# Filler and step banks counted apart, attention loads a tile ahead, C rows of 384 columns, the first step prepared first

## The chip, the cores and the metric

One core of a Trainium2 chip runs the whole program in one launch. The metric is the device time of one execution in microseconds (us). Engines are called as in the profile: PE (TensorE, matmuls), PEld (its weight loads), DVE (VectorE), ACT (ScalarE), POOL (GpSimd), SP (SyncE, which issues nearly all DMAs here). Everything below is of one core.

## The reference

The input x is 4 images of 512 channels by 64x64 positions. Two layers are added to it in turn.

```python
# layer 0: x = x + conv_ref(gn(x)); per position a layer norm over 512 channels, four chunks of 128 channels,
# each through a "mamba" (state 16, inner width 256, conv of 4 taps), a layer norm, a 512x512 projection
xz = in_proj(x);  xi, z = split(xz)
xc = silu(conv4(xi) + conv_b)
dt, Bs, Cs = split(xc @ x_proj_w.T);  dt = softplus(dt @ dt_proj_w.T + dt_proj_b)
h = exp(dt * A) * h + (dt * x) * B        # a scan over 4096 positions, for 256 channels x 16 states
y = sum_over_states(h * C)
y = (y + xc * D) * silu(z);  out = y @ out_proj_w.T
# layer 1: x = x + attn(gn(x)): linear attention with relu, 8 heads of 64
q, k, v = gn(x) @ w_qkv.T + b_qkv;  q, k = relu(q), relu(k)
kq = sum_over_positions(k^T q)  per head;   out = (v kq / kq.sum) @ w_out.T + b_out
```

gn is a group norm over a whole image. So the attention of an image can begin only when layer 0 has finished that whole image, and its second half only when kq has been summed over all positions.

## The kernel before

**Steps and slots.** Positions go in tiles of 512. A step is one chunk of 128 channels of one tile: 4 images x 8 tiles x 4 chunks = 128 steps (`steps`, `n`). A step has 16 slots (`SLOTS`, `s`); `slot` runs two scans (L596), and the next DVE product with the C row (`product`, L619, columns 0 to 383; the last 128 columns are multiplied by POOL, L607, with rows that come by DMA). For the scans ACT makes exp(dt A) in PSUM (`decay`, L570) and POOL makes dt x B (`drive`, L578). `c_row` spreads a row of C over the partitions by a bf16 matmul into a PSUM bank of its own (`ps_c`, 1 buffer), once every two slots, right behind the product that used the row before. `fold_states` sums the states by matmul into `y`.

**Around a slot.** The loop over steps is recorded in a fixed order (`manual_schedule`), engine by engine. Behind each slot, `after()` records the work of the next steps at set slots: `front` (the conv `pc`, two pieces each, and `pz`, of step n+2), `silu`, `mix` and `last_mix` (the piecewise `mixers`: `pd`, its copy to `dt` and `parts`, and two rounds of `minus` matmul and copy that split `parts` into bf16 pieces), `time_banks` (`pt`), `time_steps` (softplus, between two loads of ACT's table), `spread`, `gate`, `out_proj` (`po`), `with_skip`.

**Fillers.** What is not bound to a slot stands in four queues of generators and gets at most one piece per slot each: `ahead` (norm of the next tile), `late` (the layer norm and projection `pp` of the tile just done, `leave`), `rest` (attention), `light` (statistics of the next image). A generator yields "wait" when it can't go on: `room()` waits for a PSUM bank, `until()` for a piece that was recorded `later(2, ...)`, two slots on, `load()` for one of three x tiles (`TILES`), `pause(2)` for two slots. `credit` limits the matmuls per slot. Four PSUM banks (`ps_w`, `work_bank`, `free`, `held`) serve steps and fillers alike.

```python
limit[0] = 2 if s in (SLOTS - 1, 0, 5, 6) else BANKS - 1     # BANKS = 4; compared with held[0], all banks in use
```

**Attention of one image** (`attention`, in queue `rest`): pass a, over 8 tiles of 4 sub-tiles: load the tile (`xa`), pause, group norm on ACT, and for each sub-tile q and k (`pq`, a bias matmul and 4 f32 matmuls each), relu on ACT, and the sums k^T q (`pk`, 8 matmuls of 64x64, which read both relus), added to `kq` on DVE. Then a middle part (`pm2`, `pm3`, `pob`) folds kq and the weights into one 512x512 matrix. Pass b, over 8 tiles: load (`xb`), four outputs of 4 matmuls (`pr`), ACT adds the offset, SP stores.

**Before and behind the loop.** Before the loop, steps 0 and 1 are prepared (`step_inputs`, `silu`, `mixers`), then step 0's rows are spread and the first drives and decays are made. Behind the loop, the queues `late` and `rest` are simply emptied: `while late or rest: one(late) or one(rest)`; there a scheduler, and not the recorded order, places the instructions, `now[0]` is None, and nothing waits for a slot.

Of the kernel before, what the change touches and what calls it, by code (L numbers as in the profile page):

```python
# [24 lines left out]
def kernel(  # L25
# [49 lines left out]
    BANKS = 4  # L75
# [3 lines left out]
    def work_bank(name):  # L79
        held[0] += 1  # L80
        return ps_w.tile([P, T], F32, tag="w", name=name)
# [25 lines left out]
    def room():  # L107

        while now[0] is not None and held[0] >= limit[0]:
            yield "wait"  # L110

    limit, norming = [BANKS], []
# [11 lines left out]
    def load(src, name):  # L124

        while now[0] is not None and held_x[0] >= TILES:
            yield "wait"
        held_x[0] += 1
        xt = wk.tile([P, NC, T], F32, tag="x", name=name, bufs=TILES)
        nc.sync.dma_start(xt, src)  # L130
        return xt

# [193 lines left out]
    def layer_norm(v, name, gained):  # L326


        def means(parts, what, when):
            yield from room()  # L330
            sums = work_bank(f"{what}_sums_{name}")
            for c in range(NC):
                mm(
                    sums[c * LANE : (c + 1) * LANE, :], ones, parts[c],
                    start=True, stop=True, abreast=NC,
                )
            got = wk.tile([P, T], F32, tag="sq", name=f"{what}_got_{name}", bufs=4)

            def take():
                nc.scalar.copy(got, sums)  # L340
                free()

            copied = later(2, take)
            yield
            yield from until(copied)
            yield when
            yield from room()
            bank = work_bank(f"{what}_{name}")
            mm(bank, mean.to_broadcast([P, P]), got, start=True, stop=True)
            return bank  # L350

        while norming:
            yield "wait"
        norming.append(name)
        mu = yield from means([v[:, c, :] for c in range(NC)], "mu", "one ahead")
        yield "wide"
        nc.vector.tensor_tensor(v, v, bc(mu, NC), ALU.subtract)
        free()
        yield "free"
        sqs = []  # L360
        for c in range(NC):
            sqs.append(wk.tile([P, T], F32, tag="sq", name=f"sq_{name}_{c}", bufs=4))
            nc.scalar.activation(sqs[c], v[:, c, :], AF.Square)
            if c == 1:
                yield "free"
        var = yield from means(sqs, "var", "two ahead")
        rs = wk.tile([P, T], F32, tag="sq", name=f"rs_{name}", bufs=4)

        def root():
            nc.scalar.activation(rs, var, AF.Ln, bias=eps)  # L370
            nc.scalar.activation(var, rs, AF.Exp, scale=-0.5)

        rooted = later(2, root)
        yield
        yield from until(rooted)
        yield "wide"
        nc.vector.tensor_tensor(v, v, bc(var, NC), ALU.mult)  # L377
        free()
        norming.clear()
        yield  # L380
        if gained:
            for c in range(NC):
                nc.scalar.activation(
                    v[:, c, :], v[:, c, :], AF.Identity,
                    bias=b_sb[:, c : c + 1], scale=g_sb[:, c : c + 1],
                )
                if c % 2:
                    yield "free"
# [45 lines left out]
    def inputs(f, xn, c, nm):  # L434
# [11 lines left out]
        def take(e):  # L446
            nc.scalar.activation(xz[:, 0, e, :], pc[e], AF.Identity, bias=cb[:, e : e + 1])
            free()

        for e in range(NH):  # L450
            pc[e] = work_bank(f"pc_{nm}_{e}")
            taps(e, range(NTAP // 2))
            yield
            taps(e, range(NTAP // 2, NTAP))
            later(2, lambda e=e: take(e))
            yield
        for e in range(NH):
            pz = work_bank(f"pz_{nm}_{e}")
# [5 lines left out]
            def take_z(e=e, pz=pz):  # L464
                nc.scalar.copy(xz[:, 1, e, :], pz)  # L465
                free()

            later(2, take_z)

    def time_banks(f, nm):  # L470

        f["pt"] = [work_bank(f"pt_{nm}_{e}") for e in range(NH)]
# [4 lines left out]
    def time_steps(f, nm):  # L477
# [4 lines left out]
        free(NH)  # L482
# [18 lines left out]
    def mixers(f, nm):  # L501
# [3 lines left out]
        pd = work_bank(f"pd_{nm}")  # L505
# [12 lines left out]
        parts = f["parts"] = wk.tile([P, T], BF16, tag="parts", name=f"parts_{nm}", bufs=2)  # L518
        nc.scalar.copy(parts, pd)
        for i in (2, 3):  # L520
            yield
            mm(pd, minus, parts, start=False, stop=True, skip_group_check=True)
            yield
            nc.scalar.copy(parts[i * LANE :, :], pd[i * LANE :, :])  # L524
        free()
# [33 lines left out]
    def c_row(g):  # L559
        n, e, q, _ = place(g)  # L560
        got = ps_c.tile([P, T], F32, tag="c", name=f"c_all_{g}")
# [52 lines left out]
    def product(g, last):  # L614
# [4 lines left out]
        nc.vector.tensor_tensor(own, own, bc(c_all[g // JJ][:, :CUT], 2), ALU.mult)  # L619
# [27 lines left out]
    def out_proj(f, nm):  # L647
        f["po"] = work_bank(f"po_{nm}")
# [3 lines left out]
    def with_skip(f, xn, c):  # L652
        v = xn[:, c, NTAP - 1 : NTAP - 1 + T]
        nc.vector.scalar_tensor_tensor(v, v, sk, f["po"], ALU.mult, ALU.add)
        free()
# [13 lines left out]
    def attention(b, x1s, norm):  # L669
# [4 lines left out]
        qk = both[:, 1:3, :].rearrange("p j c -> p (j c)")  # L674

        def relu(j, pq):
            nc.scalar.activation(qk[:, j * C : (j + 1) * C], pq, AF.Relu)  # L677
            free()
# [8 lines left out]
        for t in range(NT):  # L687
            gn = yield from load(x1s[t], f"xa_{b}_{t}")
            yield
            yield from pause(2)  # L690
            yield "free"
            yield from group_norm(gn, gn, norm)
            for u in range(SUB):
                nm = f"{b}_{t}_{u}"
                ready = []
                for j in range(2):
                    yield from room()
                    pq = work_bank(f"pq_{nm}_{j}")
                    mm(
                        pq, sel[:, 0, 0:1].to_broadcast([P, P]), bqk[:, j * C : (j + 1) * C],  # L700
                        start=True, stop=False,
                    )
                    for c in range(NC):
                        mm(
                            pq, gn[:, c, u * P : (u + 1) * P], w_qk[:, c, j * C : (j + 1) * C],
                            start=False, stop=(c == NC - 1),
                        )
                        if c == 1:
                            yield "more"
                    ready.append(later(2, lambda j=j, pq=pq: relu(j, pq)))  # L710
                    yield
                yield from until(*ready)
                yield from room()

                pk = work_bank(f"pk_{nm}")[:, 0 : C // 2].rearrange("p (c d) -> p c d", c=NC)
                for p in range(NC):
                    for i in range(P // HEAD):
                        r = slice(p * P + i * HEAD, p * P + (i + 1) * HEAD)
                        mm(
                            pk[i * HEAD : (i + 1) * HEAD, p, :], qk[:, r], qk[:, C:][:, r],  # L720
                            start=(p == 0), stop=(p == NC - 1), skip_group_check=True,
                        )
                if u == SUB - 1:
                    later(1, free_x)
                added = later(2, lambda pk=pk, first=(t + u == 0): add(pk, first))
                yield
# [54 lines left out]
        yield from until(*taken)  # L781
        ob = small.tile([P, NC], F32, tag="ob", name=f"ob_{b}")
# [33 lines left out]
        for t in range(NT):  # L816
            x1 = yield from load(x1s[t], f"xb_{b}_{t}")
            yield
            yield from pause(2)
            for o in range(NC):  # L820
                yield from room()
                pp = work_bank(f"pr_{b}_{t}_{o}")
                for m in range(NC):
# [4 lines left out]
                    if m == 1:  # L828
                        yield "more"
                if o == NC - 1:  # L830
                    later(1, free_x)
                later(2, lambda t=t, o=o, pp=pp: store(t, o, pp))
# [32 lines left out]
    def leave(b, t):  # L865
# [8 lines left out]
        if t == NT - 1:  # L874
            yield
            norms[b, 1] = stats_end(stats1[b], f"b{b}")
            add_to(rest, attention(b, x1s[b], norms[b, 1]))
            yield
# [30 lines left out]
    for n in range(2):  # L909
        run(step_inputs(n))  # L910
        silu(n)
    run(mixers(fs[0], names[0]))
    time_banks(fs[0], names[0])
# [4 lines left out]
    run(mixers(fs[1], names[1]))  # L918
    nc.scalar.preload_act_table_set("natural_log_exp_and_others")
    for g in range(0, 3 * JJ, JJ):  # L920
        b_row(g)
    c_tail(0)
    c_row(0)
    for g in range(2):
        drive(g)
    for k in range(LEAD):
        decay(k)

    with tc.manual_schedule():
        credit, mix, held[0], held_x[0] = 0.0, iter(()), 0, 0  # L930
        for n, (b, t, c) in enumerate(steps):
# [10 lines left out]
            for s in range(SLOTS):  # L942
                def after():
# [10 lines left out]
                    if s < 3:  # L954
# [11 lines left out]
                    if s in (2, 4, 5, 6, 7):  # L966
# [10 lines left out]
                    if s == 5 and before is not None:  # L977
                        pb_, pt_, pc_ = steps[n - 1]
                        with_skip(before, xn[pb_, pt_], pc_)
                        if pc_ == NC - 1:  # L980
                            add_to(late, leave(pb_, pt_))
# [3 lines left out]
                    if s >= 13:  # L985
# [7 lines left out]
                    limit[0] = 2 if s in (SLOTS - 1, 0, 5, 6) else BANKS - 1  # L993
# [76 lines left out]
```

## Time and profile before

| | us |
|---|---|
| three runs | 8470.25, 8464.2, 8470.84; median 8470.25 |
| the profiled execution, its own time | 8479.35 |
| its span, first to last instruction | 8477.6 |
| busy: DVE / POOL / PE / ACT | 7348.7 / 6860.0 / 6672.1 / 5274.0 |
| first scan starts / last scan starts | 120.38 / 7840.67 |

The profile gives the shares of busy time in 40 slices of 212 us. The loop with its scans fills slices 1 to 37; the last slices hold attention alone. A line of the timeline or of the chain of waits begins with the start in us from the first instruction and the duration. Of the groups, a line gives the busy time, the mean duration of one in ns and the idle time of the engine before them, with what ended most of it. One f32 matmul of the source (128x512) stands in the trace as two matmul rows.

### The profile page before, as it was taken

How to read it: one execution, taken by the hardware profiler on the slowest of the kernel's cores; microseconds unless marked ns; L12 is line 12 of the kernel's file. 1: busy time of each engine (PE TensorE's matmuls, PEld its weight loads, DVE VectorE, ACT ScalarE, POOL GpSimd, SP SyncE). 2: the span in 40 equal slices, each digit the busy share in tenths (PEclk: the TensorE clock that was granted, in tenths of full speed). 3: DMA queues.
4: the chain of work that ended last, by engine and by line, in shares of the span. 5: the costliest groups of instructions: out<-in, count | busy, mean ns of one | idle time of the engine just before them, and what ended most of it. 6: DMA issues, size and time to landing. Idle time of an engine off the chain costs nothing. (4 is left out here: it accounts for less than half of the span.)

```text
span 8477.6 us, 86763 instructions
## 1 busy us (share of the span) xinstructions
PE 6672.1 (79%) x22169; PEld 2222.3 (26%) x22240; DVE 7348.7 (87%) x7097; ACT 5274.0 (62%) x7584; POOL 6860.0 (81%) x4565
## 2 busy tenths in 40 slices
PE   5677677777788888888888778888788888787999
PEld 1112121111222222222222222222222222222444
DVE  5999999999999999999999999999989999999000
ACT  4666666666666666666666766666666666665221
POOL 4999998999888888888888888888888898888000
PEclk8777787777888888888889998898888898888999
DMA  5666666566666665567666666566666666665202
GB/s 156 160 152 155 152 155 151 144 149 147 157 163 159 148 162 144 146 156 184 174 169 159 161 154 149 148 153 153 162 167 173 143 159 149 153 149 142 104 30 85
DMA packets 829304, 1266.14 MB, mean 149 GB/s; under 512 B 183920, under 2 KB 317568, under 8 KB 816512
## 3 DMA queue, kind: packets, MB, share of 16 engines
q1 hardware_dynamic: 821632, 1255.87, 59.3%
q10 hardware_dynamic: 7168, 4.71, 0.2%
q8 instruction: 174, 2.85, 0.2%
q14 instruction: 330, 2.70, 0.1%
HBM read 1053.28 MB, written 206.57 MB: 149 GB/s over the span
## 5 line engine op out<-in xcount | busy, mean ns | idle before, releaser
L578 POOL TENSOR_TENSOR bx<-d_all,b_all 128x1024 f32<-128x1024 f32 x2048 | 4795.8, 2360 | 113.6 <-DVE h L596 97.4
L596 DVE TENSOR_TENSOR_SCAN h<-dA,st,bx 128x512 f32<-128x512 f32 x3584 | 4457.2, 1274 | 273.5 <-ACT dA L570 199.7
L570 ACT ACTIVATE dA<-d_all,a_t 128x512 f32<-128x512 f32 x4096 | 2800.5, 689 | 2384.2 <-DVE h L596 2371.6
L619 DVE TENSOR_TENSOR h<-h,c_all 128x768 f32<-128x768 f32 x2048 | 1915.7, 935 | 73.2 <-PE c_all L120 63.8
L120 PE MATMUL c_all<-parts,sel 128*128 128x512 bf16 x1024 | 458.8, 448 | 1252.6 <-DVE h L619 1250.5
L120 PE MATMUL y<-h,fold 128*32 128x512 f32 x8192 | 1378.0, 752 | 62.0 <-POOL h L607 60.7
L607 POOL TENSOR_TENSOR h<-h,c_sb 128x512 f32<-128x512 f32 x1024 | 1298.1, 1268 | 116.1 <-DMA c_sb<-c_rows 29.0
L120 PE MATMUL pc<-xn,w_cv 128*128 128x512 f32 x2048 | 1051.6, 645 | 21.4 <-ACT parts L524 13.8
L120 PE MATMUL pq<-w_qk,xa 128*128 128x512 f32 x2048 | 980.5, 608 | 8.7 <-issue 6.6
L606 POOL COPY st<-h 128x4 f32<-128x4 f32 x1024 | 192.4, 188 | 638.1 <-DVE h L596 589.5
L596 DVE TENSOR_TENSOR_SCAN h<-dA,bx 128x512 f32<-128x512 f32 x512 | 605.3, 1211 | 92.1 <-POOL bx L578 48.0
L120 PEld LDWEIGHTS <-sel 128*128 128x128 bf16 x1280 | 126.2, 99 | 2125.8 <-DVE h L619 1944.6
L120 PEld LDWEIGHTS pc<-xn,w_cv 128*128 128x128 f32 x2048 | 396.2, 206 | 742.8 <-issue 650.0
L120 PEld LDWEIGHTS pq<-w_qk,xa 128*128 128x128 f32 x2048 | 397.8, 196 | 483.1 <-issue 471.0
L120 PE MATMUL pp<-xn,w_pr 128*128 128x512 f32 x1024 | 516.5, 633 | 7.5 <-DVE xn L377 3.8
L120 PE MATMUL pr<-xb,m 128*128 128x512 f32 x1024 | 495.5, 629 | 13.8 <-ACT xz L465 7.1
L120 PE MATMUL y<-xz,dg 128*128 128x512 f32 x512 | 391.2, 858 | 0.0
L120 PEld LDWEIGHTS y<-h,fold 128*32 128x32 f32 x8192 | 175.8, 118 | 686.7 <-issue 400.1
L643 POOL TENSOR_TENSOR xz<-xz 128x512 f32<-128x512 f32 x256 | 325.0, 1270 | 1.8 <-ACT xz L640 1.8
L487 POOL TENSOR_TENSOR dt<-dt,xz 128x1024 f32<-128x1024 f32 x128 | 302.5, 2363 | 24.4 <-ACT dt L479 24.4
L677 ACT ACTIVATE kq<-pq 128x512 f32<-128x512 f32 x256 | 150.2, 587 | 247.0 <-PE pq L120 246.5
L120 PE MATMUL pd<-parts,minus 128*128 128x512 bf16 x256 | 121.0, 473 | 230.3 <-ACT parts L524 147.7
(151 smaller groups left out, 6159.4 us busy)
## 6 DMA issues: line engine op xcount, KB each, us to landing
d_all<-d_rows SPq DMA_DIRECT2D x2048, 256.0 KB, 6.6
b_all<-b_rows SPq DMA_DIRECT2D x4096, 64.0 KB, 2.2
d_rows<-dt SPq DMA_DIRECT2D x256, 512.0 KB, 3.4
c_sb<-c_rows SPq DMA_DIRECT2D x4096, 16.0 KB, 1.8
xs<-in_x_dram SPq DMA_DIRECT2D x32, 1024.0 KB, 7.7
xn<-in_x_dram SPq DMA_DIRECT2D x32, 1024.0 KB, 6.0
xr<-in_x_dram SPq DMA_DIRECT2D x32, 1024.0 KB, 6.9
x<-xr SPq DMA_DIRECT2D x32, 1024.0 KB, 4.2
```

The costliest lines, as they stand in the source:

```text
L120: nc.tensor.matmul(out_, lhsT, rhs, **how)
L487: nc.gpsimd.tensor_tensor(f["both"][:, 1], f["both"][:, 0], f["xz"][:, 0], ALU.mult)
L570: nc.scalar.activation(dAs[k], fs[n]["d_all", e][:, 0, j, :], AF.Exp, scale=a_t[:, e, j, q : q + 1])
L578: nc.gpsimd.tensor_tensor(bxs[g], fs[n]["d_all", e][:, 1, jj * 2 : jj * 2 + 2, :], bc(b_all[g // JJ], 2), ALU.mult)
L596: nc.vector.tensor_tensor_scan(h[:, j, :], dAs.pop(2 * g + i), bxs[g][:, i, :], 0.0 if t == 0 else st[:, c, e, q, j : j + 1], ALU.mult, AL ...
L606: nc.gpsimd.tensor_copy(st[:, c, e, q, :], h[:, :, T - 1])
L607: nc.gpsimd.tensor_tensor(h[:, :, CUT:], h[:, :, CUT:], bc(c_sb.pop(g // JJ), NJ), ALU.mult)
L619: nc.vector.tensor_tensor(own, own, bc(c_all[g // JJ][:, :CUT], 2), ALU.mult)
L643: nc.gpsimd.tensor_tensor(f["xz"][:, 1, e, :], f["xz"][:, 1, e, :], f["xz"][:, 0, e, :], ALU.mult)
L677: nc.scalar.activation(qk[:, j * C : (j + 1) * C], pq, AF.Relu)
```

## The change

The diff, cut to what is spoken of. The step's own banks are no longer counted; fillers count theirs, against a new limit. In attention the x tiles are fetched by the piece before they are needed, and the sums of a sub-tile are recorded behind the next sub-tile's q (three relu buffers instead of two). The statistics of an image are ended inside `attention`, behind the first fetch. The C row, `parts` and their matmuls have 384 columns. `with_skip` is recorded before the conv piece of its slot, `pz` is cut in two pieces (slots 7 and 8), and `mix` starts one slot earlier. Before the loop, step 0 goes the whole way before step 1 is begun.

```diff
-    BANKS = 4
-    def work_bank(name):
-        held[0] += 1
+    def work_bank(name, behind=1):
+        held[0] += behind
...
+    def no_tile():
+        return now[0] is not None and held_x[0] >= TILES
+
+    def load_now(src, name):
         held_x[0] += 1
         xt = wk.tile([P, NC, T], F32, tag="x", name=name, bufs=TILES)
         nc.sync.dma_start(xt, src)
         return xt
...
-            pc[e] = work_bank(f"pc_{nm}_{e}")
+            pc[e] = work_bank(f"pc_{nm}_{e}", 0)
...
+            later(2, lambda e=e, pz=pz: nc.scalar.copy(xz[:, 1, e, :], pz))
+            yield
...
-        parts = f["parts"] = wk.tile([P, T], BF16, tag="parts", name=f"parts_{nm}", bufs=2)
-        nc.scalar.copy(parts, pd)
+        parts = f["parts"] = wk.tile([P, CUT], BF16, tag="parts", name=f"parts_{nm}", bufs=2)
+        nc.scalar.copy(parts, pd[:, :CUT])
...
-        got = ps_c.tile([P, T], F32, tag="c", name=f"c_all_{g}")
+        got = ps_c.tile([P, CUT], F32, tag="c", name=f"c_all_{g}")
...
+        def fetch(t, why):
+            if t < NT and t not in tiles and not no_tile():
+                x1 = load_now(x1s[t], f"x{why}_{b}_{t}")
+                tiles[t] = x1, pause(2)
+
+        def fetched(t, why):
+            fetch(t, why)
+            while t not in tiles:
+                yield "wait"
+                fetch(t, why)
+            x1, landing = tiles.pop(t)
+            yield from landing
+            return x1
...
-        for t in range(NT):
-            gn = yield from load(x1s[t], f"xa_{b}_{t}")
-            yield
-            yield from pause(2)
...
-                yield from until(*ready)
-                yield from room()
...
+        fetch(0, "a")
+        yield
+        norm = stats_end(stats, f"b{b}")
+        yield
+        for v in range(NT * SUB):
+            t, u = divmod(v, SUB)
...
+                qk[i] = both[:, 1 + i % 3, :]
+                ready[i] = later(2, lambda i=i, pq=pq: relu(i, pq))
+                if u:
+                    fetch(t + 1, "a")
...
+                if v and j == 0:
+                    yield from sums(v - 1)
                     yield
...
+        fetch(0, "b")
...
-            x1 = yield from load(x1s[t], f"xb_{b}_{t}")
-            yield
-            yield from pause(2)
+            x1 = yield from fetched(t, "b")
...
+                fetch(t + 1, "b")
...
-    for n in range(2):
-        run(step_inputs(n))
-        silu(n)
+    run(step_inputs(0))
+    silu(0)
     run(mixers(fs[0], names[0]))
+    b_row(0)
+    c_tail(0)
...
     for g in range(2):
         drive(g)
+    run(step_inputs(1))
+    silu(1)
+    run(mixers(fs[1], names[1]))
...
-                    if s < 3:
+                    if s < 2:
                         next(last_mix, None)
...
-                    if s in (2, 4, 5, 6, 7):
+                    if s in (2, 4, 5, 6, 7, 8):
                         next(front, None)
...
-                    if s >= 13:
+                    if s >= 12:
                         next(mix, None)
...
-                    limit[0] = 2 if s in (SLOTS - 1, 0, 5, 6) else BANKS - 1
+                    limit[0] = 3 if 9 <= s < 13 else 2
```

## The prediction, made before the changed kernel had run

> **What bounds the kernel now.** I read first the busy shares over the 40 slices, to see which engine sets the pace where:
>
> ```profile
> PE   5677677777788888888888778888788888787999
> DVE  5999999999999999999999999999989999999000
> ```
>
> For 37 slices DVE is at nine tenths and sets the pace; then it is at nothing, and PE at nine tenths is alone. So there are two kernels to price: a loop of 2048 slots bound by DVE, where matmuls cost only what they delay, and a stretch behind it bound by PE. The chain of waits that ended last shows what stands in that stretch:
>
> ```profile
> 7899.11 2.31 issue
> 7901.42 19.10 PE pm L120 x40
> 7920.52 11.08 PE pob L120 x64
> 7931.59 112.56 PE pr L120 x256
> 8044.17 5.65 DMA xa<-x
> 8049.85 2.22 ACT xa L315 x3
> ```
>
> An image has one middle part and 256 rows of `pr`, and here they come twice: before 8044 they are those of image 2, whose attention was not done when the loop ended; image 3 begins only at 8049.85. Third, the windows by image (columns: window, its length, then busy us and count of PE, PEld, DVE, ACT, POOL, granted clock, DMA share, GB/s):
>
> ```profile
> 120.00:2002.00 1882.00, 1326.91 (x4030) 365.35 (x4030) 1799.61 (x1696) 1232.30 (x1748) 1710.81 (x1136) 0.78 0.63 152
> 2002.00:3949.00 1947.00, 1567.98 (x5373) 519.58 (x5391) 1837.61 (x1766) 1300.83 (x1874) 1715.20 (x1140) 0.86 0.63 156
> 3949.00:5901.00 1952.00, 1573.31 (x5394) 520.16 (x5410) 1833.98 (x1759) 1308.00 (x1887) 1715.92 (x1141) 0.88 0.64 159
> 5901.00:7844.00 1943.00, 1564.41 (x5348) 521.47 (x5371) 1804.82 (x1713) 1278.06 (x1844) 1708.24 (x1135) 0.88 0.63 155
> ```
>
> DVE is idle for window less busy: 82, 109, 118 and 138 us. Image 0 has no attention beside it; the three others have one each, and pay 27, 36 and 56 us of idle DVE for it. Last, whom DVE waits for in these three images (us in total, times, longest):
>
> ```profile
> DVE h L596 <- ACT dA L570: 181.2, 103, 4.9
> DVE h L619 <- PE c_all L120: 63.8, 58, 4.3
> DVE h L596 <- POOL h L607: 27.6, 25, 1.8
> ```
>
> ACT's exp that comes late is the first, the C row that stands behind other matmuls the second.
>
> **Part 1, image 2's attention leaves the end.** I counted in the order of the two built programs' PE instructions, by C rows (1024, one for two slots). Before, pass a of images 0, 1 and 2 begins at C rows 284, 565 and 853; each takes some 280 rows for the 256 that an image has, so it falls behind, and at row 1024 the last sums, the middle part and all of pass b of image 2 are left. After, they run over rows 282 to 466, 538 to 722 and 794 to 976: 184 rows each, ending 48 rows early. So the removed waits (two slots for the relus of each sub-tile, load and pause for each tile, room that step banks took away) are real, and the left-over goes. Image 3's start is then set by its own group norm:
>
> ```profile
> 7888.61 0.16 DVE L309 TENSOR_TENSOR off_b<-ngm_b,gr_b 128x4 f32<-128x4 f32 x1 [1.12 <-POOL gr_b L305]
> ```
>
> It is ready at 7888.77, and ACT starts its first tile at 8049.82: with the load of tile 0 issued before the statistics, these 161 us go. The cover is the loop; its price is part 4.
>
> **Part 2, sums behind the next q, at the end.** In pass a of image 3 each sub-tile takes 8.83 us (two are 17.67 in the chain), and holds one stall:
>
> ```profile
> 8096.78 0.69 PE L120 MATMUL pk<-kq 128*64 128x64 f32 x16 [0.74 <-ACT kq L677]
> ```
>
> `pk` waits 0.74 us for the relu of its k. Behind the next q, some 4 us later, that relu (0.60 us) is done. 31 of 32 sub-tiles have a next q: 31 x 0.74 = 23 us, all on the path, since PE alone is busy there. ACT has 51 us of work in these 274 us and can't become the bound; the middle part and pass b (112.8 us of `pr` without a gap) stay.
>
> **Part 3, step 0 first.** Step 1's matmuls and copies stood before step 0's `dt` copy; silu of step 0 ends at 89.47 and that copy starts at 96.68. So step 0's rows go out some 5 us earlier. But ACT now does step 1's copies and silu before the first exps, which came at 114.12: by my count from the durations there they come at about 115.5, and the first scan at about 116.5 instead of 120.38. I take 4 us off; ends are 8 off (drive alone decides) and 2 on.
>
> **Part 4, the loop.** (a) PE gets 172 units more (a unit is one f32 128x512 matmul of the source): 1315 instead of 1143 of attention, and it gets them denser: some 51 units per step over some 70 steps, where before 46 were spread over 92; then 26 steps have none. Busiest before were steps of 53 units:
>
> ```profile
> 5042.00:5105.00 63.00, 54.69 (x177) 18.53 (x176) 60.25 (x60) 40.43 (x57) 53.36 (x35) 0.86 0.60 144
> ```
>
> There PE is busy 54.7 of 63 us, 1.03 us a unit, and DVE idles 2.8 us: no more than the 2.6 us of a step without attention (82 / 32). So density as such costs little, and I take 0. Bounds: attention costs 119 us of idle DVE now (27 + 36 + 56). If none were left, 119 off. If all 70 steps idled like the worst tile, the first of image 3 (four steps, 26.6 us):
>
> ```profile
> 5900.70:6152.90 252.20, 202.97 (x650) 69.40 (x651) 225.64 (x229) 160.53 (x230) 214.77 (x143) 0.84 0.65 162
> ```
>
> that is 6.6 less 2.6, so 4.0 us a step, 280 us, less the 119: 161 on.
>
> (b) ACT. The usual late exp follows the burst in slot 2:
>
> ```profile
> 825.75 0.58 ACT L524 CAST parts<-pd 32x512 bf16<-32x512 f32 x1
> 826.35 1.28 ACT L963 ACT_TABLE_LOAD   x1
> 827.64 1.26 ACT L479 ACTIVATE dt<-pt,dtb 128x512 f32<-128x512 f32 x2
> 828.93 1.28 ACT L965 ACT_TABLE_LOAD   x1
> ```
>
> With `mix` a slot earlier, the `parts` copy leaves this burst. 91 of the 128 steps stall at slot 4; taking at most 0.58 off each stall gives 50 us. It is given back elsewhere: the second `pz` copy (0.58) moves from slot 9 into the burst of slot 10, before silu (1.28 + 1.91 + 1.28), where 0.58 more costs about 30 by the same sum, and the copy comes back in slot 1, about 10. Net 10 off; ends 50 off and 40 on. The queues passed are ACT's and PE's own; `b_rows` and `c_rows` go to SP a slot earlier, which nobody waits for.
>
> (c) C rows: 1024 x 448 ns shrink by a quarter, 115 us of PE time, off the path; the 58 waits on `c_all` lose about 0.11 us each, 6 us, within (a). Bank waits: by bank and order, a bank taken in the slot in which its last user frees it occurs 229 times after, 270 before: nothing. (d) Image 2's middle part now takes some 4 us of DVE time in the loop: 4 on. (e) A fetch recorded early can hold up SP, with the rows of the next steps behind it, only if its tile is still being read; fetches go only when one of three tiles is free by count: 0.
>
> **A rule of the skill beside a row.** The granted clock is 0.78 in image 0, 0.86 to 0.88 beside attention and 1.00 in the last pass a: a denser PE is a faster PE. The Trainium skill, "TensorE: Matmul & The Clock Gate" (section "What's actually happening"), says that the array runs at half rate by default and after an idle window of about 3.4 us, and at full rate only after as long a busy one. That speaks against the 26 steps now left without filler. By it a unit there would cost about 1.76 us (an estimate: the page's halving, applied to the 112.56 / 256 = 0.44 us of a `pr` row at the end, two rows a unit), 49 us for their 28 units, still under a step of 57; the sum would stay the same.
>
> **Sum.** 161 + 23 + 4 + 10 off, 4 on: 194 off. The profiled execution (8479.35, 1.75 around its span) would be 8285; the median of the runs is 9.1 lower: 8470.25 - 194 = 8276.
>
> **Rivals.** (A) The forecast: the loop costs between 80 off and 40 on: 8200 to 8322. (B) The gain at the end is there, but the crowded steps stall DVE: between 40 and 161 on, 8322 to 8443. For it: image 3's first tile; against: the 53-unit steps. (C) PE becomes the bound of the crowded steps: slower than before. A step beside attention takes 1947 / 32 = 60.8 us. At the whole trace's mean for a matmul row (`pr` 629 ns, `pp` 633), a unit is 1.26 us, 51 units are 64.3 us, 3.5 us more than a step has; 70 times is 245 on, against 188 off at the ends: 8527. It decides from 2.7 us a step, a unit of 1.245 us; against it stand the 1.03 us in the busiest steps. (D) The waits move elsewhere and image 2 still isn't done in the loop: 8276 + 161 = 8437; the order of the program speaks against it.
>
> **Chances.** A 0.66, B 0.26, C 0.06, D 0.02. The range 8200 to 8370 holds nearly all of A and over half of B; it leaves out the rest of B, C and D. About 0.2% (17 us) is what a measurement of this kernel can tell from no change. Faster: A, nearly all of B, D: 0.92; same 0.02; slower, C: 0.06.
>
> **What would show it.** Right: `pm` and 256 `pr` once behind the last scan, the first group norm of image 3 within some 6 us of the last `pp`, no stall before `pk`, DVE idle in the loop at 400 to 500 us. Wrong: waits on `c_all` well over 64 us (B, C), images 1 to 3 longer than 1947, or late exps at slot 12 in most steps.

## The result and the profile after

| | before | after |
|---|---|---|
| median (range), runs | 8470.55 (8464.2 to 8472.71), 4 | 8461.37 (8460.75 to 8468.05), 4 |
| profiled execution: span | 8477.6 | 8459.3 |
| start: to the first scan | 120.4 | 125.2 |
| loop: first scan to last scan | 7720.3 | 7877.0 |
| end: last scan to the last instruction | 637.0 | 457.1 |

After over before is 0.9992, with a 95% interval of 0.9975 to 1.0009: no difference that this measurement can tell. The forecast was 8276, its range ended at 8370, and it gave 0.02 to this outcome. But the small difference is a sum of large ones: the end is 179.9 us shorter, the loop 156.7 us longer, the start 4.8 us longer.

First the two rows that opened the reading of before, the busy shares in 40 slices:

```profile
PE   5667676667788888876788888886678888887599
DVE  5999999999999998889989999889999999889800
```

The end without DVE has shrunk from three slices to two. But DVE's row, 9 almost throughout before, now has 8s in groups, at slices 16 to 18, 26 to 27 and 35 to 36 above all: once per image with attention beside it. The chain that ended last (start, duration, what):

```profile
8311.07 0.61 ACT kq L694
8311.72 0.71 PE pk L120 x16
...
8314.78 18.88 PE pm L120 x40
...
8342.84 112.83 PE pr L120 x256
```

There is one middle part and one set of 256 `pr`, those of image 3; only the last `pk`, which has no next q, still waits for a relu. The loop by image, in the same windows and columns as before the change:

```profile
125.20:2004.60 1879.40, 1280.49 (x4030) 358.69 (x4030) 1801.25 (x1696) 1225.07 (x1749) 1706.04 (x1133) 0.79 0.62 152
2004.60:4011.70 2007.10, 1616.96 (x5552) 546.74 (x5552) 1838.15 (x1767) 1305.43 (x1896) 1715.78 (x1139) 0.88 0.62 157
4011.70:6025.90 2014.20, 1619.14 (x5552) 546.50 (x5552) 1838.43 (x1767) 1305.42 (x1896) 1716.02 (x1139) 0.88 0.62 157
6025.90:8006.00 1980.10, 1576.28 (x5489) 531.85 (x5489) 1809.29 (x1721) 1276.43 (x1855) 1708.91 (x1136) 0.88 0.61 154
```

Window less DVE's busy time is 78, 169, 176 and 171 us, 594 in all, where before it was 447. Image 0, without attention, is as good as before; the others idle 60, 58 and 33 us more. That is 147 of the loop's 157 us; DVE's own busy time is some 11 us more. Whom DVE waits for in images 1 to 3:

```profile
DVE h L596 <- ACT dA L570: 276.6, 175, 5.4
DVE h L619 <- PE c_all L120: 101.3, 80, 5.0
```

Late exps cost 95 us more than before (181.2), late C rows 38 us more (63.8). Put down to slots from the trace (idle DVE in images 1 to 3, before to after): slot 4 156 to 72, slot 12 41 to 97, slot 15 35 to 136, slot 3 26 to 67, slot 7 0 to 47. So the question for the experiments is what came to slot 15, and what to slots 3 and 7.

**Slot 15: a wait for a buffer.** The waits of ACT over the loop, for the `parts` copy: the row of before, then that of after.

```profile
ACT parts L519 <- PE c_all L120: 24.1, 23, 2.3
```

```profile
ACT parts L520 <- PE c_all L120: 242.1, 126, 4.3
```

The copy writes `parts`, and what it waits for is a C row: a reader of `parts`. There are two buffers (`bufs=2`). The copy for step n+2 takes the buffer of step n, and the last C row of step n (for slots 14 and 15) is recorded in slot 14. With `mix` begun at slot 12 the copy is recorded at slot 13, ahead of that row. ACT works in order, so it stands there. One of the 126, by ACT's and then DVE's timeline (start, duration; in brackets the idle time before and its releaser):

```profile
3045.18 0.48 ACT L520 CAST parts<-pd 128x384 bf16<-128x384 f32 x1 [0.75 <-PE c_all L120]
3045.55 1.52 ACT L321 ACTIVATE xa<-xa,off_b,gr_b 128x512 f32<-128x512 f32 x2
3046.97 1.28 ACT L570 ACTIVATE dA<-d_all,a_t 128x512 f32<-128x512 f32 x2
```

```profile
3047.75 1.28 DVE L596 TENSOR_TENSOR_SCAN h<-dA,st,bx 128x512 f32<-128x512 f32 x1 [1.81 <-ACT dA L570]
```

The copy stands 0.75 us for `c_all`; two group norms of attention and the exps are behind it, and DVE waits 1.81 us for the exp. The releaser in DVE's row is ACT; only ACT's own waits show that the cause is PE's reading.

**Slot 3: a wait for a PSUM bank, and a C row behind it.** PE's waits over the loop:

```profile
PE pt L120 <- ACT res L842: 44.6, 11, 4.3
PE pt L120 <- ACT kq L694: 33.5, 12, 4.2
PE pt L120 <- ACT parts L525: 28.2, 19, 2.5
```

With two smaller rows (on DVE, 21.0 us) these are 49 waits and 127 us. None of these rows is in before, where the waits of `pt` add up to 0.5 us. `pt` is recorded at slot 1 and takes two of the four work banks. While the step's own banks were counted, a filler could not hold a bank that `pt` needed; now it can, and `pt` stands until `res` or `kq` (the copies of a filler's bank) or the last `parts` copy (of `pd`'s bank) is done. PE in one such place, then DVE:

```profile
3316.59 2.07 PE L120 MATMUL pt<-dt,w_dt 32*128 32x512 f32 x2 [4.32 <-ACT res L842]
3318.59 3.78 PE L120 MATMUL pr<-xb,m 128*128 128x512 f32 x4
3322.16 0.53 PE L120 MATMUL c_all<-parts,sel 128*128 128x384 bf16 x1
```

```profile
3322.73 0.95 DVE L619 TENSOR_TENSOR h<-h,c_all 128x768 f32<-128x768 f32 x1 [2.17 <-PE c_all L120]
```

PE stood idle 4.32 us for a bank, the next C row came behind `pt` and four `pr` rows, and DVE lost 2.17 us. Of the 104 us that DVE waits for C rows in images 1 to 3, 41 are at slot 3 (24 waits), and all 24 have a stand of `pt` in the 8 us before them.

**Slot 7: no bank, but a full PE.** Another 46 us of the waits for C rows are at slot 7 (36 waits), and none of these has a stand of `pt` before it. PE simply has no gap there, as these rows of PE and then of DVE show:

```profile
2209.62 1.88 PE L120 MATMUL pc<-xn,w_cv 128*128 128x512 f32 x4
2211.34 1.88 PE L120 MATMUL pq<-w_qk,xa 128*128 128x512 f32 x4
2213.05 0.33 PE L120 MATMUL c_all<-parts,sel 128*128 128x384 bf16 x1
```

```profile
2213.42 0.95 DVE L619 TENSOR_TENSOR h<-h,c_all 128x768 f32<-128x768 f32 x1 [3.37 <-PE c_all L120]
```

The C row stands behind pieces of attention (`pq`) that alternate with the step's conv (`pc`). In 44 of the 46 us PE has no gap of over 0.1 us in the 8 us before. Before the change DVE had no such wait at slot 7; with the step's banks counted, the conv's own banks left a filler less room ahead of this C row (experiment 8 puts that back).

**And pass b is the dearest stretch.** Windows of image 1: pass a (16 steps), the middle part and nearly all of pass b (7 steps), steps without attention (4):

```profile
2183.95:3175.60 991.65, 844.76 (x3118) 296.18 (x3119) 916.95 (x880) 668.00 (x975) 857.31 (x568) 0.92 0.61 153
3175.60:3642.24 466.64, 391.16 (x1251) 139.37 (x1250) 405.83 (x385) 292.07 (x427) 375.57 (x250) 0.90 0.66 174
3776.60:4011.70 235.10, 161.42 (x512) 45.39 (x512) 224.65 (x210) 153.87 (x220) 213.66 (x142) 0.79 0.60 149
```

Window less busy per step: 4.7 us in pass a (74.7 / 16), 8.7 in pass b (60.8 / 7), 2.6 without attention. Pass b idles nearly twice as much as pass a, though PE is no busier in it (0.84 of the window against 0.85): it is not PE's load as a whole.

### The profile page after: what moved, and what is told of

The parts are those of the page before. It is cut to its first block, busy times and chain, and to the rows that moved or that the text cites. A ratio compares the mean times of both kernels' runs of the same rounds, so it can differ in the third digit from the quotient of the medians.

```text
span 8459.3 us, 87042 instructions
## 1 busy us (share of the span) xinstructions
PE 6579.8 (78%) x22240; PEld 2204.0 (26%) x22240; DVE 7355.8 (87%) x7097; ACT 5239.5 (62%) x7585; POOL 6861.1 (81%) x4565
## 5 line engine op out<-in xcount | busy, mean ns | idle before, releaser
L619 DVE TENSOR_TENSOR h<-h,c_all 128x768 f32<-128x768 f32 x2048 | 1909.7, 932 | 110.5 <-PE c_all L120 101.3
L120 PE MATMUL c_all<-parts,sel 128*128 128x384 bf16 x1024 | 386.3, 377 | 1454.8 <-DVE h L619 1453.4
L120 PE MATMUL pc<-xn,w_cv 128*128 128x512 f32 x2048 | 1028.6, 631 | 21.8 <-ACT res L842 14.9
L120 PE MATMUL pq<-w_qk,xa 128*128 128x512 f32 x2048 | 1008.5, 625 | 1.1 <-ACT xa L321 1.1
L120 PE MATMUL pr<-xb,m 128*128 128x512 f32 x1024 | 515.8, 643 | 0.5 <-ACT xz L469 0.3
L120 PE MATMUL pt<-dt,w_dt 32*128 32x512 f32 x512 | 272.7, 889 | 128.8 <-ACT res L842 44.6
L120 PE MATMUL y<-xz,dg 128*128 128x512 f32 x512 | 363.3, 801 | 0.0
L120 PE MATMUL pd<-xz,w_xp 128*128 128x512 f32 x512 | 304.9, 726 | 7.8 <-ACT xz L911 7.8
```

Source lines behind the costliest of these rows:

```text
L120: nc.tensor.matmul(out_, lhsT, rhs, **how)
L619: nc.vector.tensor_tensor(own, own, bc(c_all[g // JJ], 2), ALU.mult)
```

## The experiments

The causes in question were three: the buffer, the uncounted banks, and the crowding of pass b's outputs. In the expectations, theory W is the wait for the buffer, and D says that density makes PE and ACT late; from experiment 5 on, K is the wait of `pt` for a bank, and D2 the crowding of pass b. The rivals were that the moved copies as such burden ACT (then another buffer gives nothing), and that PE is simply fuller (then counting and buffers give nothing). All ratios are against the kernel before on the same chip, with 95% intervals; before was 8468.27 to 8470.66 there.

**1. A third buffer for `parts`, everything else as after.**

```diff
-        parts = f["parts"] = wk.tile([P, CUT], BF16, tag="parts", name=f"parts_{nm}", bufs=2)
+        parts = f["parts"] = wk.tile([P, CUT], BF16, tag="parts", name=f"parts_{nm}", bufs=3)
```

> The changed kernel with three buffers for the parts of C instead of two, nothing else. Theory W (a wait for a buffer): with mix one slot earlier, ACT's copy into parts must wait for the last C row of the running step, which still reads that buffer; the late exps at slot 15 (1.29 us a step in images 1 to 3, 0.47 in image 0, 139 us together) come from it. Then the waits of that copy on C rows (242 us on ACT, 126 times) fall to near nothing and the time falls by 80 to 140 us, to 8320 to 8380. Theory D (density): the crowded attention makes PE and ACT late and the wait only shows up where they are late anyway; then the time falls by less than 30 us, to above 8430.

Measured: 8376.33 us, ratio 0.9888 (0.9873 to 0.9903): 85 us less than after, as theory W had it. ACT's waits have no row `parts` on `c_all` any more, idle DVE at slot 15 falls from 136 to 32 us, and the loop from 7877.0 to 7794.6 at the same end (457.7). The copy's place is unchanged, so it was the buffer and not ACT's load. Not all of the 104 us at slot 15 came back: waits for C rows grew from 101.3 to 148.2 us, since they had partly been hidden behind the late exps.

**2. `mix` back at its old slots, two buffers.**

```diff
-                    if s < 2:
+                    if s < 3:
                         next(last_mix, None)
...
-                    if s >= 12:
+                    if s >= 13:
                         next(mix, None)
```

> The changed kernel with mix back at slot 13 and its last piece back in slot 2, as before the change. Theory W: the wait at slot 15 goes (139 us off), but the parts copy is back in the softplus burst, so that the stall at slot 4 comes back (some 60 to 90 us on): 8380 to 8420. Theory D: less than 30 us in either direction, 8430 to 8490.

Measured: 8507.21, ratio 1.0045 (1.003 to 1.006): a miss. The buffer wait is as small as before (20.9 us) and slot 15 is mended (39 us), yet it is 46 us slower than after. DVE's waits in images 1 to 3, and one of PE's rows over the loop, tell most of why:

```profile
DVE h L619 <- PE c_all L120: 237.7, 134, 5.0
```

```profile
PE pt L120 <- ACT parts L525: 55.1, 12, 4.6
```

`mix` a slot later ends at slot 2, behind `pt`, so `pd`'s bank is still held when `pt` takes its banks; idle DVE at slot 3 goes from 67 to 173 us. 43 of the 49 waits for C rows at slot 3 (105 of 127 us) have a stand of `pt` in the 8 us before. So without the earlier `mix` the rest of the change costs more.

**3. Only the earlier `mix`, in the kernel before.**

```diff
-                    if s < 3:
+                    if s < 2:
                         next(last_mix, None)
...
-                    if s >= 13:
+                    if s >= 12:
                         next(mix, None)
```

> The kernel before with mix one slot earlier (12 instead of 13, last piece in slot 1), nothing else. Theory W: the copy's wait appears here as well, in all 128 steps, with no denser attention: late exps at slot 15 of 0.5 to 1.3 us a step (60 to 160 us) against some 50 us off at slot 4: 8480 to 8570. Theory D: the wait costs little where attention is thin: 8420 to 8470, the forecast's 10 to 50 off.

Measured: 8513.68, ratio 1.0051 (1.0036 to 1.0066), 43 us slower; the loop is 41.5 us longer. Slot 4 gains (156 to 119 us), slot 15 loses (35 to 120), and ACT waits 208.2 us for C rows at the `parts` copy. So this part of the change alone, with two buffers, is a loss of its own, as theory W had it.

**4. Pass b spread out: two slots of pause behind each `pr` output in the loop.**

```diff
+                if now[0] is not None:
+                    yield from pause(2)
```

> The changed kernel with a pause of two slots behind each output of pass b inside the loop; by the program's order pass b then takes 72 C rows instead of 45 and still ends 21 rows before the loop does. Theory D: the steps of pass b, which idle DVE by 6 to 14 us each now, fall to 4 to 5; some 27 steps less 4 us and some more steps beside thin attention: 60 to 110 off, 8350 to 8400. Theory W: the late exps at slot 15 stay; 10 to 40 off, 8420 to 8450.

Measured: 8406.95, ratio 0.9917 (0.99 to 0.9933): 54 us less than after, between the two forecasts. Steps 53 to 57 of image 1 take 306 us instead of 335, and pass b still ends inside the loop.

**5. Third buffer and spread together.** The edits of 1 and 4.

> Three parts buffers and the pause of two slots behind each output of pass b together. The two took 85 and 55 us off one by one. Theory D2 (what is left beside the buffer's wait is the crowding of pass b): they add up, 8310 to 8340. Theory K (what is left is the wait of pt for a bank that a filler still holds at slot 1, which keeps C rows behind it; in the program's order such a bank is freed no slot earlier for 57 of the pt banks here, as in the kernel without the pause): pass b's spreading gives little more, 8345 to 8375.

Measured: 8329.69, ratio 0.9829 (0.9814 to 0.9844). With the third buffer the spreading gives 47 us, without it 54: the two nearly add.

**6. Third buffer, and fillers kept to one bank at slot 0.**

```diff
-                    limit[0] = 3 if 9 <= s < 13 else 2
+                    limit[0] = 3 if 9 <= s < 13 else 1 if s == 0 else 2
```

> Three parts buffers, and only one bank for fillers at slot 0 (2 before), so that pt at slot 1 finds a free bank more often (36 instead of some 50 to 60 with no slot between, by the program's order); attention keeps its pace (pass b takes 48 C rows instead of 45). Theory K: the waits of pt on banks (130 us on PE) and the 96 us of idle DVE at slot 3 fall by a third or more: 25 to 45 us off the 8376, 8330 to 8350. Theory D2: 8365 to 8380.

Measured: 8329.15, ratio 0.9833 (0.9818 to 0.9848): 47 us off experiment 1. `pt` then waits 26.7 us for `parts` and 40.3 for `res`, and no longer for `kq`; but the fillers' `pq` now stands for the `parts` copy too (54.4 us in 12 waits, 1.6 in experiment 1). Idle DVE at slot 3 falls from 95 to 61 us, and at slot 7 it stays (53 and 54). One limit at one slot is worth as much as the spreading.

**7. All three.** The edits of 6 and 4.

> All three: three parts buffers, one filler bank at slot 0, the pause in pass b. Theory D2: as with the first and the last alone, 8310 to 8340. Theory K: as with the first two, 8330 to 8350. Both at once: 8290 to 8320. The loop then takes 7720 to 7740 us, as before the change, and the 180 us at the end stay.

Measured: 8303.80 (8301.92 to 8304.5), ratio 0.9802 (0.9788 to 0.9817). The loop is 7715.9 us, where that of before was 7720.3, and the end stays at 458.6. The limit and the spreading overlap: alone each gives 47 us, together 73. `pt` still waits 44.4 us for `parts` and 26.4 for `res`.

**8. The old counting.** Step banks counted again, with the old limits; with three buffers, and with two.

```diff
-            pc[e] = work_bank(f"pc_{nm}_{e}", 0)
+            pc[e] = work_bank(f"pc_{nm}_{e}")
...
-        f["pt"] = [work_bank(f"pt_{nm}_{e}", 0) for e in range(NH)]
+        f["pt"] = [work_bank(f"pt_{nm}_{e}") for e in range(NH)]
...
-                    limit[0] = 3 if 9 <= s < 13 else 2
+                    limit[0] = 2 if s in (SLOTS - 1, 0, 5, 6) else 3
```

> Three parts buffers, with the old counting: all banks counted, the limit 2 at slots 15, 0, 5 and 6, else 3. Attention then takes some 246 C rows an image, and about half of image 2's pass b is left behind the loop (some 55 us of pr). pt finds a bank freed in the same slot 18 times. Theory K and D2 alike: the loop falls by 50 to 80 us against the kernel with three parts buffers alone, to 7715 to 7745, and the end is 50 to 65 us longer: 8350 to 8390, the same time by another split. If the loop stays at 7790, neither banks nor crowding is what is left.

> The changed kernel with the old counting of banks alone (two parts buffers): the fourth corner of counting and buffers. New counting costs 64 us with three buffers (8376 against 8312); the buffer's wait costs 85 with the new counting. If the two are independent: 8312 + 85 = 8397. If the wait at slot 15 is hidden where PE and ACT are less crowded: 8320 to 8350. If it costs more by itself, as in the kernel before with mix at 12 (43 slower than before in spite of 35 us less at slot 4): about 8400.

Measured: 8312.07 with three buffers, ratio 0.9811 (0.9795 to 0.9828), and 8425.59 with two, 0.9952 (0.9938 to 0.9966). Both miss their forecasts: the first is 38 us below its range, the second above all of its three values. The four corners:

| | 2 buffers | 3 buffers |
|---|---|---|
| new counting | 8461 | 8376 |
| old counting | 8426 | 8312 |

The buffer costs 85 us with the new counting and 114 with the old; the counting costs 36 and 64. They are not independent, and no one number belongs to either. Nor is the counting a matter of bank waits alone: this edit brings back the old limits and a slower attention as well. With three buffers it takes idle DVE at slot 3 from 95 to 31 us and at slot 7 from 53 to 9, but at slot 4 from 74 up to 141. With three buffers and the old counting, `pt`'s waits are gone (0.7 us), and the waits of DVE's product for C rows fall to 13.4 us (63.8 before; with those put down to scans, 33 against 64).

The loop is 7696.9, shorter than that of before (7720.3); but attention is slower again (image 2's pass b reaches to the last C row by the order of instructions), and the end is 487.4 instead of 457.7. So the old counting gives up 30 us at the end for 98 in the loop.

**9. The old start, on the last version with three buffers.** The start before the loop as it was (steps 0 and 1 prepared together).

> Old counting, three parts buffers, and the start as before the change (steps 0 and 1 prepared together). The first scan starts at 125.3 with the new start and at 120.4 in the kernel before: if the new start costs what it seems, the first scan is at 119 to 122 and the time 3 to 6 us below 8312. If the late first scan comes from something else (the narrower C rows, the order of the rows' DMAs): 124 to 126, and no change.

Measured: 8315.33 (8306.5 to 8322.83), ratio 0.9822 (0.9808 to 0.9835): no difference to 8312 that can be told. The first scan is at 123.1, 2.2 us before that with step 0 first; too little to show in a total. That lies between the two forecasts, and nearer to the second.

**10. As 9, with one more bank for fillers at slot 6.**

```diff
-                    limit[0] = 2 if s in (SLOTS - 1, 0, 5, 6) else 3
+                    limit[0] = 2 if s in (SLOTS - 1, 0, 5) else 3
```

> The same (old counting, three buffers, old start), with the limit 3 instead of 2 at slot 6: by the program's order pass b of image 2 then runs to the loop's very end, and 15 pt banks are freed in the same slot. If the loop stays at 7697 and the end falls from 487 to 460: 8275 to 8290. If the bank at slot 6 is one that a step bank waits for: the loop is 20 or more longer and the time 8300 or above.

Measured: 8293.56 (8287.61 to 8300.61, 5 runs), ratio 0.9797 (0.9783 to 0.981), the lowest median: 175 us under before on the same chip and 168 under after. The end is back at 453.5, but the loop is 7716.5, 20 us longer than in experiment 8, so the time lies between the two forecasts. Experiment 7 has 8303.80, and the intervals of the two ratios overlap: counting the step's banks, or keeping fillers small where the step takes its banks, can't be told apart by these runs.

## Why the prediction was wrong, and where right

**The end (parts 1 and 2): right.** 161 + 23 = 184 was forecast, 179.9 came. ACT's first group norm of image 3 starts 49.6 us after the last scan instead of 209.1, so 159.6 of the 161, and 5.7 us after the last `pp` (8046.04 to 8051.76; "within some 6 us" was the mark). From there on a sub-tile takes 8.02 us (7.40 + 0.62 in the chain) instead of 8.83: 31 x 0.81 = 25 us for the stall before `pk`. From image 3's first group norm to the last instruction it is 407.5 us instead of 427.8, 20 less where 23 were forecast.

**The start (part 3): wrong in sign.** 4 us off was forecast, 4.8 on came. The count put the first exps at 115.5. ACT's timeline of after:

```profile
111.16 1.91 ACT L911 ACTIVATE xz<-xz 128x2048 f32<-128x2048 f32 x1
116.98 0.58 ACT L512 COPY dt<-pd 64x512 f32<-64x512 f32 x1 [3.92 <-issue]
...
124.37 1.30 ACT L570 ACTIVATE dA<-d_all,a_t 128x512 f32<-128x512 f32 x2
```

I had added up durations of step 1's work, but it is a chain through PE: silu of step 1, `pd`, its copy, and two rounds of `minus`, with 3.92, 2.22 and 1.96 us of waiting between. All of it now stands ahead of the first exp on ACT. The size rests on one profile of each kernel: over all profiles the first scan is at 120.4 to 123.1 with the old order (four profiles) and at 123.7 to 125.7 with the new (nine), so the sign holds, and the size is some 3 to 5 us.

**The loop (part 4): wrong, and here the forecast fell.** Forecast 6 off with bounds -80 and +161; measured +157.

- Step (b), "the copy comes back in slot 1, about 10", is the term that failed most. Its two other terms went the way forecast: in images 1 to 3, slot 4 lost 84 us of idle time (50 forecast), slot 12 gained 56 (30). Not all of that is their doing. The earlier `mix` alone took 37 us off slot 4 (experiment 3), and with the old counting slot 4 is back at 135 to 141 in spite of it, so the larger part of the 84 goes with the new counting and its limits. Slot 12 gained 34 with the old counting, and the `pz` copy was not put back alone. The step failed elsewhere: I followed the moved copies through the engines' queues alone. The copy also takes a buffer, and its last reader stands behind the slot that the copy was moved ahead of. By experiments 1 and 8 that is 85 to 114 us. It could have been foreseen: before already showed 23 waits of this copy for `c_all` at one slot later, the buffer count is in the line, and the order of instructions puts the copy ahead of the row.
- Step (c), "229 times after, 270 before: nothing", counted bank waits over all banks and takers. What mattered was which matmul takes the bank. `pt` has the next C row behind it, and it stood for a bank 49 times after (127 us), once before (0.5 us). The sum over all takers fell while the one with DVE behind it rose. By the corners, the counting, with its limits and its denser attention, cost 36 to 64 us; how much of that is bank waits (slot 3) and how much is fillers let in ahead of a C row (slot 7) is not separated. The C rows' own time fell by 73 us (458.8 to 386.3), not 115, and gave nothing that the waits show.
- Step (a), density at nothing, took the 53-unit steps of before for typical. They were steps in which the step's banks were still counted. In after, the 46 us of idle DVE at slot 7 come with a PE that has no gap: there density costs by itself, though no experiment takes away slot 7 alone. Pass b cost 47 to 54 us by experiments 4 and 5; part of that is the same bank wait (experiment 4 takes the waits for C rows at slot 3 from 41 to 15 us), so how much of it is crowding alone stays open.
- Step (d): 4 forecast for image 2's work on DVE, 11 more busy time came.

The marks for "wrong" that I set did show two of three: images 1 to 3 longer than 1947, and waits on `c_all` well over 64 us. Late exps rose most at slot 15, not 12; at slot 12 there are 59 in 96 steps (13 before).

**The rivals.** B (the crowded steps stall DVE, 8322 to 8443) had the right place and sign, and its upper bound for the density, 161, happens to lie by the measured 157; but the measured total, 8461, is above its range, and over half of the loss was not load: the third buffer alone took 82 of the loop's 157 us. How much of the other 74 is load is open; slot 7 and the spreading of pass b say that it is not nothing. Once the buffer, the limit and the spreading are mended (experiment 7), the loop costs nothing any more and the time is 8304, inside the forecast's own range of 8200 to 8322. C fell: PE did not become the bound; in pass b it is busy for 391 of 467 us. D fell too: pass b is done in the loop.

**The rule of the clock.** In the four steps without attention the granted clock is 0.79 and DVE idles 2.6 us a step, as before without filler; in pass a it is 0.92 and in pass b 0.90. The Trainium skill, "TensorE: Matmul & The Clock Gate" (section "What's actually happening"), has the clock fall where PE idles; the direction agrees, and it cost nothing here, since PE is busy for 161 of 235 us at that clock. The skill's "Perfetto Trace Analysis" (section "Optimization Strategy") says that the same gap repeating on the engine that should be saturated can mean too few buffers for the next tile. That fits the 126 repeated waits of the `parts` copy. Here the gap on DVE, the saturated engine, named ACT's exp, and the buffer showed one engine further back, in ACT's own waits.

**Not settled.** The fetch a tile ahead, the 384 columns and the sums behind the next q were not undone one at a time. That together they bring image 2's attention forward is seen from the order, and the shorter end of all versions that have them shows it (453 to 487 us against 637); what each gives is not measured. What slot 12 gained is left in every one of these versions, too.

## What to carry to other kernels

When an instruction is moved earlier, look at what it writes as well as at its queue: count the buffers, and find the last reader of the buffer it takes in the recorded order. When a shared resource is no longer counted, ask of each taker what stands behind it in its engine's queue, and not how often waits occur in all; ask as well what the freed room lets in ahead of the row that the busiest engine waits for. A total that does not move may hide gains and losses of 150 us; cut the span where the bound changes before looking for causes.

## What the runs showed of the hardware

A quarter fewer columns did not take a quarter off a matmul: the median `c_all` went from 390 ns (512 columns) to 337 ns (384), 14%, and the shortest from 376 to 322 ns. And a wait that is taken away can uncover another one: without the buffer wait, waits for C rows rose from 101.3 to 148.2 us, so that 104 us less at one slot were worth 82 us of loop.
